# Layer 1 of a four-layer graph network: gate operations that read their scores in PSUM, and one-hots' buffers in another pool

## The chip, the cores and the metric

The kernel runs on one core of a Trainium2 chip. The core has a matrix engine (TensorE, PE in the profile; its weight loads are the rows PEld), a vector engine (VectorE, DVE), a scalar engine (ScalarE, ACT), a general engine (GpSimd, POOL) and a queue engine that starts DMA transfers (SyncE, SP). Each engine works through its own instructions in order, and engines wait for each other by semaphores. SBUF is the on-chip memory that all engines and the DMA read and write; PSUM holds the matmuls' results and can be read and written by VectorE and ScalarE too. The metric is device time in microseconds (us), as a median over several executions. Times inside a profile come from one further execution with the profiler.

## The reference, cut to what matters

An array `x` of 8 batches, 2048 nodes and 64 features, in float32, goes through four layers, each `x = layernorm(x + GNN_k(x))`. Layers 0, 2 and 3 are graph products with the adjacency `adj` (2048 x 2048, rows normalised) and with weights; layer 1, which the change touches, is an attention over 64 hyperedges:

```
h    = x @ W
agg  = softmax over the hyperedge's nodes of leaky_relu(h @ a_node), applied to h   # [b, e, f]
beta = sigmoid((h @ a_gn)[node] + (agg @ a_ge)[hyperedge])
all_he = elu(beta * h + (1 - beta) * agg)                       # per node and hyperedge
coefs1 = softmax over a node's hyperedges of tanh(elu(agg) @ fcW + fcb) @ av
g        = sum over hyperedges of coefs1 * all_he
industry = (adj / deg) @ (x @ W_ind)
out = industry and g, mixed by a softmax over tanh(. @ fcW + fcb) @ av
x   = layernorm(x + out)
```

A node belongs to few hyperedges, three on average: one drawn, and each of the others with a probability of 3%.

## The kernel before

**Data.** Rows are cut into 16 tiles of 128 nodes (`NT` = 16, `P` = 128); a tile holds all batches and features side by side, 8 x 64 = 512 columns (`BC`). The adjacency lies as 0/1 masks in DRAM scratch, 1 MB for a tile, and comes back through SP as `mj_l1_<tile>`. A product with it is 16 x 2 matmuls of 128 x 512 for a tile (line L1399 in layer 1), since the operand is split into a high and a low part.

**Stages.** The first product of layer 0 also prepares, beside its matmuls, what layer 1 needs of the hyperedges: for each tile four one-hot matrices `oh` (slots 0 to 3 of a node: which hyperedge it holds), a matrix `S` for what does not fit in slots, and `pT`, all stored to DRAM. Layer 0 follows, with weights that differ by node; then layer 1; then layers 2 and 3.

**Layer 1's beginning.** One pool, `l1`, lives through the whole layer (`S`, `agg1`, `nagg`, `ext` and small constants). A second pool, `fa`, holds what the beginning alone needs (`pT`, `agg`, `he`, `rec` and others); it is closed, and the memory after it goes to the pools `fw` (small tiles of the units, allocated by `small`) and `mjp` (two masks). A tile of `fw` or `mjp` can therefore be loaded only after the last reader of what lay at its address. The beginning loads `pT` and `S` in four parts each (`S` through SP behind a flag that VectorE computes at L1451, which decides between this program and a general one), forms `agg` (L537) and a copy of it in two parts (L545 is one of these copies), the scores of hyperedges with matmuls and exponentials (L575, L578 and L579 are small VectorE operations on [128 x 8] of them), sums into `ext`, a product `dnp` with `pT`, and last `hgr`, two numbers per node and batch: the node's part of the gate, and the reciprocal of the softmax's sum (L599). The part of tile 0's `industry` that can be done early runs on TensorE between these steps.

**Units.** `units(j)` computes `g` of tile j. It loads `oh` (L632, buffers for 4 tiles), and forms scores in one PSUM bank, `sm`: four matmuls one-hot x `ext` (L636), one of `S` x `hgr` (L640) and a transpose of `S` (L154). So each of the 80 score columns is a sum or a product partner for a slot u, a kind k (0: gate, 1: coefficient) and a batch. ScalarE copies the transpose to `ST` (L647) and the 80 columns to `ex` in SBUF (L649). VectorE makes `gate` (kind 0, add) and `coef` (kind 1, multiply), two operations each: slots 0 to 2 with `hgr` (24 columns, L654) and the last slot from two columns of `ex` (8 columns, L658). ScalarE turns `gate` into `sig` and `rest` (step `tau`, L661 to L665). POOL multiplies `h` by `sig` (L680, `ch0`, `ch1`), TensorE looks up `agg` with the one-hots (`gp0`, `gp1`, L693), VectorE multiplies that by `rest` and adds (`z`: L700, L703), ScalarE takes exp (L705) and a product for the last slot (`t3`, L718, eight small ones), VectorE forms the elu `ez` (`e`, L723), POOL multiplies by `coef` and sums (`w` and `ga`: L725, L729, L731), and a matmul with `ST` adds the last slot (`red`, L734; L736).

**Industry and mixer.** `industry(j)` is the 32 matmuls with the mask, steps `i`, and then `ind` (L754) and `dlt` (L758). `mix_and_norm(j)` transposes `g` and `ind`, multiplies by `fcW` (`fc0`, `fc1`, L793), takes tanh (`th0` L788, `th1` L796), subtracts (`sub`, L798), multiplies by `av` (`df`, L802, 16 matmul instructions of one column), and from there weights, residual and layernorm follow (`sw` L808, `mult` L810, `r` L814, `s` L817, `centre` L819, `sq` L824, `var` L827, `rstd`, `x2` L835). `df` and the scores of a unit take turns in the same PSUM bank.

**Order.** Everything on PE, VectorE, ScalarE and POOL in layer 1 runs in the order in which it is written (`program_order()`). The turns interleave tiles by a list written by hand. In turn t, `p` is the industry of tile t, `q` its end for tile t-1, `u` the unit of tile t+1, `v` the first steps of unit t+2, `s` the end of unit t, and `m`, `o`, `f` the mixers of tiles t-1, t-2, t-3:

```
"q.ind u.gp0 u.z0 q.dlt m.xg m.tr0 v.sx m.sT0 v.ST u.exp0 u.ch1 m.fc0 m.tr1 u.dp "
"o.mult m.sT1 p.i m.th0 f.rstd u.t3 u.e0 p.i o.r m.fc1 v.gates u.w0 o.s u.gp1 p.i "
"v.tau p.i m.th1 u.z1 s.ga p.i v.ch0 u.exp1 m.sub u.e1 o.centre s.red u.w1 f.x2 p.i "
"m.df s.g o.sq m.sw o.var p.i p.i"
```

So on VectorE the order around the gates is: `r` of tile t-2, the gates of unit t+2, `s`, z1 of unit t+1, `sub` of tile t-1. On TensorE, `df` stands behind six of the eight pairs of `industry`. Before turn 0 the units 0 and 1 are filled in ("the fill"). DMAs are not in this order: SP's instructions are placed by the framework's scheduler.

Of the kernel before, what the change touches and what calls it, by code (L numbers as in the profile page):

```python
# [8 lines left out]
F32 = mybir.dt.float32  # L9
# [8 lines left out]
B, N, C, E, D, K, J = 8, 2048, 64, 64, 16, 3, 128  # L18
P = 128
# [32 lines left out]
def kernel(  # L52
# [28 lines left out]
    nc = tc.nc  # L81
# [420 lines left out]
    def layer1(  # L502
# [7 lines left out]
        l1 = stack.enter_context(tc.tile_pool(name="fl1", bufs=1))  # L510
# [104 lines left out]
        def small(tag, name, shape=(P, B), bufs=2):  # L615
            return fw.tile(list(shape), F32, tag=tag, name=name, bufs=bufs)
# [10 lines left out]
        def units(j, dst):  # L627

            oh = small("oh", f"oh_{j}", (P, 4, P), 4)
            nc.sync.dma_start(oh, lists["oh"][j // 4][:, j % 4])  # L632
            sm = ps_s.tile([P, QW], F32, tag="sm", name=f"sx_{j}")

# [10 lines left out]
            yield "sx"  # L645
            ST = small("ST", f"ST_{j}", (P, P), 3)
            nc.scalar.copy(ST, sm[:, 0:P])  # L647
            ex = small("ex", f"ex_{j}", (P, 5, 2, B))
            nc.scalar.copy(ex.rearrange("p u k b -> p (u k b)"), sm[:, P:P + 80])  # L649
            yield "ST"  # L650
            gate = small("gate", f"gate_{j}", (P, 4, B))
            coef = small("coef", f"coef_{j}", (P, 4, B), 3)
            for t, k, op in ((gate, 0, ALU.add), (coef, 1, ALU.mult)):
                nc.vector.tensor_tensor(  # L654
                    t[:, 0:3, :], ex[:, 0:3, k, :],
                    hgr[:, j, k, :].unsqueeze(1).to_broadcast([P, 3, B]), op,
                )
                nc.vector.tensor_tensor(t[:, 3, :], ex[:, 3, k, :], ex[:, 4, k, :], op)  # L658
            yield "gates"

            nc.scalar.activation(gate, gate, AF.Tanh, scale=0.5)  # L661
# [217 lines left out]

        g_of, ind_of, dlt_of = {}, {}, {}  # L880
        unit = {j: units(j, g_of) for j in range(NT)}
        mixer = {j: mix_and_norm(j) for j in range(NT)}
        product = {j: industry(j) for j in range(NT)}
# [1247 lines left out]
```

## Time and profile before

| what | value |
|---|---|
| median of 3 runs | 1344.24 us (1344.21, 1344.24, 1349.38) |
| profiled execution | 1349.78 us, its span 1347.8 us |
| TensorE clock granted, mean | 0.96 |
| busy, share of the span | PE 95%, PEld 75%, VectorE 68%, ScalarE 28%, POOL 36% |
| layer 1, in the profiled execution | from about 734 to 1072 us, turns of 16.9 us each in the middle |
| one turn in there, busy | VectorE 15.3 us, POOL 13.0 us, ScalarE 11.3 us |

The profiled execution is one execution; its span begins with the first instruction, and about 2 us of its time lie around the span. In a row of a profile's timeline stand the start and the length in us, the engine, the line, the operation with what it writes and reads, its size, and in brackets the idle time of the engine ahead of it with the operation that ended it. "SPq" rows are SP's waits ahead of a DMA. The chain of waits goes back from the last instruction, each step to what released it. "x8" after a row means eight instructions of the kind, taken together.

### The profile page before, as it was taken

To read this page: it belongs to the slowest core of one execution; us is meant where nothing else is said; L and a number is where in the kernel's file an instruction comes from. 1 tells how busy PE (TensorE), PEld (TensorE's weight loads), DVE (VectorE), ACT (ScalarE), POOL (GpSimd) and SP (SyncE) were. 2 spreads that over 40 slices of the span, in tenths; PEclk is the share of its full clock that TensorE was granted. 3 is DMA by queue.
4 is the path that set the end of the run, shared out by engine and by line. 5 is a ranking of instruction groups with operands and counts; after the bars stand their busy time and mean duration, and the time that the engine had idled before them with its cause. 6 is when DMAs were issued, how large, how long until landed. Compare 5 with 4: busy or idle time off the path is not lost.

```text
span 1347.8 us, 19945 instructions
## 1 busy us (share of the span) xinstructions
PE 1275.1 (95%) x7708; PEld 1010.0 (75%) x7708; DVE 915.7 (68%) x1559; ACT 370.7 (28%) x853; POOL 483.8 (36%) x403
## 2 busy tenths in 40 slices
PE   6999899999999999999997599999998799999997
PEld 5777688888888888888885376666666588888885
DVE  3556378787877777777663669899984646655454
ACT  2100101111222222222212446666664511111111
POOL 2000354444444444444210667777772600000000
PEclk9999899999999999999997599999998999999999
DMA  8976632333333333331604022222220133333451
GB/s 219 269 215 182 197 112 89 104 105 104 105 104 105 105 105 105 105 105 55 256 23 152 24 75 77 91 95 94 79 78 1 49 140 125 125 120 139 171 188 72
DMA packets 100358, 157.21 MB, mean 117 GB/s; under 512 B 12832, under 2 KB 64416, under 8 KB 94112
## 3 DMA queue, kind: packets, MB, share of 16 engines
q1 hardware_dynamic: 97776, 151.65, 34.7%
q10 hardware_dynamic: 2304, 4.20, 0.8%
q8 instruction: 63, 1.03, 0.3%
q14 instruction: 39, 0.32, 0.1%
q0 software_dynamic: 176, 0.02, 0.1%
HBM read 118.08 MB, written 37.76 MB: 116 GB/s over the span
## 4 chain that ended last, share of the span: by engine, by line
PE 77%; DVE 14%; DMA 3%; ACT 2%; issue 1%; POOL 1%; SPq 0%; DVEq 0%; ACTq 0%; POOLq 0%
PE pp L1081 25%; PE a L1399 18%; PE y2p L1044 9%; PE y1p L478 7%; PE ind L1399 4%; DVE d L703 3%; PE df L802 2%; DMA xraw<-in_xn 2%; DVE gp L700 2%; DVE gate L654 2%; DVE ez L723 1%; PE try L154 1%; PE yp L1489 1%; DVE coef L658 1%; DVE th L798 1%
## 5 line engine op out<-in xcount | busy, mean ns | idle before, releaser
L1092 DVE SCALAR_TENSOR_TENSOR r<-pp,emb_sb,r 128x256 f32<-128x256 f32 x512 | 247.2, 483 | 114.9 <-PE pp L1081 101.1
L1081 PE MATMUL pp<-w_sb,xT 64*128 64x256 f32 x1024 | 160.4, 390 | 1.7 <-DVE r L1092 1.7
L1030 POOL TENSOR_TENSOR r<-xs,bn 128x256 f32<-128x256 f32 x32 | 22.7, 731 | 384.8 <-issue 245.3
L1081 PE MATMUL pp<-w_sb,y1T 64*128 64x256 f32 x1024 | 153.5, 376 | 0.0
L1081 PE MATMUL pp<-w_sb,y2T 64*128 64x256 f32 x1024 | 153.5, 376 | 0.0
L478 PE MATMUL y1p<-x_hi,m 128*128 128x512 f32 x256 | 105.9, 414 | 12.0 <-ACT x_hi L425 11.6
L1081 PEld LDWEIGHTS pp<-w_sb,xT 64*128 64x128 f32 x1024 | 94.4, 186 | 25.1 <-issue 14.9
L1081 PEld LDWEIGHTS pp<-w_sb,y1T 64*128 64x128 f32 x1024 | 99.7, 187 | 10.9
L1081 PEld LDWEIGHTS pp<-w_sb,y2T 64*128 64x128 f32 x1024 | 99.6, 187 | 11.0
L1399 PE MATMUL a<-y_hi,mj_l 128*128 128x512 f32 x256 | 102.9, 402 | 5.0 <-DMA mj_l<-mask 5.0
L1399 PE MATMUL ind<-y_hi,mj_l 128*128 128x512 f32 x240 | 104.8, 437 | 0.0
L1044 PE MATMUL y2p<-y_hi,msk 128*128 128x512 f32 x256 | 103.4, 404 | 0.0
L1399 PE MATMUL a<-y_lo,mj_l 128*128 128x512 f32 x256 | 102.7, 401 | 0.0
L478 PE MATMUL y1p<-x_lo,m 128*128 128x512 f32 x256 | 102.6, 401 | 0.0
L1044 PE MATMUL y2p<-y_lo,msk 128*128 128x512 f32 x256 | 101.5, 396 | 0.0
L1399 PE MATMUL a<-v_hi,mj_l 128*128 128x512 f32 x256 | 100.1, 392 | 0.0
L1399 PE MATMUL a<-v_lo,mj_l 128*128 128x512 f32 x256 | 100.0, 391 | 0.0
L1399 PE MATMUL ind<-y_lo,mj_l 128*128 128x512 f32 x240 | 96.7, 403 | 0.0
L725 POOL TENSOR_TENSOR ez<-ez,coef 128x1024 f32<-128x1024 f32 x32 | 69.9, 2184 | 71.3 <-DVE ez L723 69.0
L986 POOL TENSOR_TENSOR ms<-msk,srow 128x1024 f32<-128x1024 f32 x32 | 89.9, 2810 | 5.2 <-DVE ms L999 5.2
L478 PEld LDWEIGHTS y1p<-x_hi,m 128*128 128x128 f32 x256 | 49.3, 192 | 24.8 <-ACT x_hi L425 12.0
L978 DVE TENSOR_SCALAR msk<-adj 128x1024 fp32r<-128x1024 f32 x32 | 63.7, 2024 | 3.9 <-DMA adj<-in_at 3.8
(273 smaller groups left out, 2430.5 us busy)
## 6 DMA issues: line engine op xcount, KB each, us to landing
mj_l<-mask SPq DMA_DIRECT2D x47, 1024.0 KB, 4.9
raw<-in_at SPq DMA_DIRECT2D x32, 512.0 KB, 5.5
adj<-in_at SPq DMA_DIRECT2D x64, 256.0 KB, 3.6
mask<-msk SPq DMA_DIRECT2D x32, 512.0 KB, 4.4
xraw<-in_xn SPq DMA_DIRECT2D x8, 512.0 KB, 5.5
oh<-oh SPq DMA_DIRECT2D x32, 128.0 KB, 2.6
xT<-in_xt SPq DMA_DIRECT2D x16, 256.0 KB, 3.1
xs<-in_xn SPq DMA_DIRECT2D x16, 256.0 KB, 2.9
```

The lines of the kernel that those rows point to most:

```text
L478: nc.tensor.matmul(accs[q][jj], r_(m[:, t, jj * P:(jj + 1) * P]), r_(part[:, mt, :]), start=i + h + t == 0 and part is x_hi, stop=i == 3 a ...
L654: nc.vector.tensor_tensor(t[:, 0:3, :], ex[:, 0:3, k, :], hgr[:, j, k, :].unsqueeze(1).to_broadcast([P, 3, B]), op,)
L700: nc.vector.tensor_tensor(by_b(gp[:, 0:n]), by_b(gp[:, 0:n]), per_b(rest, 2 * i, n), ALU.mult)
L703: nc.vector.tensor_tensor(d, d, gp, ALU.add)
L725: nc.gpsimd.tensor_tensor(by_b(ez), by_b(ez), per_b(coef, 2 * i, 2), ALU.mult)
L802: nc.tensor.matmul(df[:, b:b + 1], th[:, b % 2, (b // 2) * P:(b // 2 + 1) * P], av_sb, start=True, stop=True,)
L978: nc.vector.tensor_scalar(r_(m), raws[j][h], 0.0, None, op0=ALU.is_gt)
L986: nc.gpsimd.tensor_tensor(ms, m, srow[j].unsqueeze(1).to_broadcast([P, 8, P]), ALU.mult)
L1044: nc.tensor.matmul(acc, r_(msk[j, mt // 8][:, mt % 8, :]), r_(part[:, mt, :]), start=mt == 0 and part is y_hi, stop=mt == NT - 1 and part ...
L1081: nc.tensor.matmul(pp[:, h, pl, :], terms[j][name][rs, 2 * bq + pl], w_sb[rs, k, dq * 4 * C:(dq + 1) * 4 * C], start=k == 0, stop=k == K - 1,)
L1092: nc.vector.scalar_tensor_tensor(rb, ppv[:, :, dd, :], emb_sb[:, j, d:d + 1], rb, op0=ALU.mult, op1=ALU.add)
L1399: nc.tensor.matmul(acc, r_(a[:, mt, :]), r_(part[:, mt, :]), start=mt == 0 and part is hi, stop=mt == NT - 1 and part is lo,)
```

## The change

Two edits, both in `units`. The 80 scores are no longer copied to SBUF by ScalarE; `ex` is now a view of the PSUM bank, and the gate operations read it there. Since the last slot's operation had two operands from `ex`, one of them is now copied to SBUF first, by VectorE, into the place of the result: there are six VectorE operations for four (line numbers of the new kernel: L653, L657, L658). And `oh` is allocated in the pool `l1`, with its four buffers, in place of `fw`; its memory is thus not shared with `fa`, and that of the later tiles moves.

```
-            oh = small("oh", f"oh_{j}", (P, 4, P), 4)
+            oh = l1.tile([P, 4, P], F32, tag="oh", name=f"oh_{j}", bufs=4)
             nc.sync.dma_start(oh, lists["oh"][j // 4][:, j % 4])
...
             ST = small("ST", f"ST_{j}", (P, P), 3)
             nc.scalar.copy(ST, sm[:, 0:P])
-            ex = small("ex", f"ex_{j}", (P, 5, 2, B))
-            nc.scalar.copy(ex.rearrange("p u k b -> p (u k b)"), sm[:, P:P + 80])
             yield "ST"
             gate = small("gate", f"gate_{j}", (P, 4, B))
             coef = small("coef", f"coef_{j}", (P, 4, B), 3)
+            ex = sm[:, P:P + 80].rearrange("p (u k b) -> p u k b", u=5, k=2)
             for t, k, op in ((gate, 0, ALU.add), (coef, 1, ALU.mult)):
                 nc.vector.tensor_tensor(
                     t[:, 0:3, :], ex[:, 0:3, k, :],
                     hgr[:, j, k, :].unsqueeze(1).to_broadcast([P, 3, B]), op,
                 )
-                nc.vector.tensor_tensor(t[:, 3, :], ex[:, 3, k, :], ex[:, 4, k, :], op)
+                nc.vector.tensor_copy(t[:, 3, :], ex[:, 4, k, :])
+                nc.vector.tensor_tensor(t[:, 3, :], ex[:, 3, k, :], t[:, 3, :], op)
             yield "gates"
```

The framework's scheduler, which places the DMAs, moves some of SP's instructions as well: `pT`'s four loads ahead of two pieces of tile 0's mask, the first four `oh` directly behind `S`, and the mask of tile 1 (`mj_l1_1`) behind the reciprocal L599, since its memory now overlaps that of `rec`. On VectorE `agg` (L537) comes ahead of the flag's operations (L1449 to L1451).

More of the change, by code (lines that the diff above doesn't have):

```diff
@@ L627, in units @@
         def units(j, dst):
-            oh = small("oh", f"oh_{j}", (P, 4, P), 4)
+            oh = l1.tile([P, 4, P], F32, tag="oh", name=f"oh_{j}", bufs=4)
             nc.sync.dma_start(oh, lists["oh"][j // 4][:, j % 4])
@@ L647, in units @@
             nc.scalar.copy(ST, sm[:, 0:P])
-            ex = small("ex", f"ex_{j}", (P, 5, 2, B))
-            nc.scalar.copy(ex.rearrange("p u k b -> p (u k b)"), sm[:, P:P + 80])
             yield "ST"
@@ L652, in units @@
             coef = small("coef", f"coef_{j}", (P, 4, B), 3)
+            ex = sm[:, P:P + 80].rearrange("p (u k b) -> p u k b", u=5, k=2)
             for t, k, op in ((gate, 0, ALU.add), (coef, 1, ALU.mult)):
@@ L657, in units @@
                 )
-                nc.vector.tensor_tensor(t[:, 3, :], ex[:, 3, k, :], ex[:, 4, k, :], op)
+                nc.vector.tensor_copy(t[:, 3, :], ex[:, 4, k, :])
+                nc.vector.tensor_tensor(t[:, 3, :], ex[:, 3, k, :], t[:, 3, :], op)
             yield "gates"
```

## The prediction

> **What bounds the kernel now.** I read the page's first part, then the chain of work that ended last in order of time (start, length, work), then the timeline of one turn of layer 1.
>
> ```profile
> PE 1275.1 (95%) x7708; PEld 1010.0 (75%) x7708; DVE 915.7 (68%) x1559; ACT 370.7 (28%) x853; POOL 483.8 (36%) x403
> 735.89 4.21 DMA oh<-oh
> 760.74 1.81 DVE coef L658
> 783.95 1.84 PE L802 MATMUL df<-av_sb,th 128*128 128x1 f32 x16
> 854.93 3.38 PE ind L1399 x8
> 915.04 1.80 DVE gate L654
> 921.94 1.95 PE df L802 x16
> 923.89 1.96 PE ind L1399 x8
> ```
>
> TensorE bounds the span, but in layer 1 (734 to 1072 us) the chain leaves it: a load of one-hots at the beginning, a gate operation of VectorE later. The fourth line is from the timeline, for use below. Now one turn in steady state:
>
> ```profile
> 914.59 2.21 POOL L725 TENSOR_TENSOR ez<-ez,coef 128x1024 f32<-128x1024 f32 x1 [1.62 <-DVE ez L723]
> 914.96 1.88 DVE L654 TENSOR_TENSOR gate<-ex,hgr 128x24 f32<-128x24 f32 x1
> 916.77 0.15 DVE L658 TENSOR_TENSOR gate<-ex 128x8 f32<-128x8 f32 x1
> 916.84 0.17 DVE L654 TENSOR_TENSOR coef<-ex,hgr 128x24 f32<-128x24 f32 x1
> 916.88 1.30 POOL L729 TENSOR_TENSOR g<-ez 128x512 f32<-128x512 f32 x1
> 916.94 1.26 DVE L658 TENSOR_TENSOR coef<-ex 128x8 f32<-128x8 f32 x1
> 919.38 1.91 POOL L680 TENSOR_TENSOR d<-h,sig 128x1024 f32<-128x1024 f32 x1
> 919.53 1.22 DVE L703 TENSOR_TENSOR d<-d,gp 128x1024 f32<-128x1024 f32 x1
> 921.11 0.40 PE L1399 MATMUL ind<-y_lo,mj_l 128*128 128x512 f32 x1
> 921.94 1.95 PE L802 MATMUL df<-av_sb,th 128*128 128x1 f32 x16 [0.44 <-DVE th L798]
> ```
>
> Two gate operations of 24 and 8 columns take 1.88 and 1.26 us where their like take 0.17, and each ends with a POOL operation (914.59 + 2.21 = 916.80, 916.88 + 1.30 = 918.18): VectorE with two operands in SBUF waits while POOL reads SBUF. L703, with one operand in PSUM (gp), runs beside POOL in its usual 1.22. So the gates' 0.43 us (L654 begins 773.30, the last L658 ends 773.73, when POOL is away) become 3.24. The `sub` operation (L798) then ends late, and df waits for it: the matmuls before it start 0.233 apart, so df could start at 921.34 and starts at 921.94.
>
> **The change, part by part.**
> 1. *Gates read PSUM.* Out go 16 copies by ScalarE (0.23 us each). They hide: in a turn ScalarE is busy 11.28 of 16.9 us, and after the copy at 927.68 it waits 1.03 us for VectorE. Worth nothing. VectorE gets six operations for four, two of which wait for the copy ahead of them. Start to start is 0.09 us without a wait and 0.21 with one (the pair L578, L579 at 728.62 and 728.83): 0, 0.09, 0.30, 0.39, 0.48, 0.69, end 0.86 us, so 0.43 more than four operations unblocked, but 2.38 less than now. Does reading PSUM cost more? The small row L575 (from PSUM) takes 0.17 us, L578 (from SBUF) 0.17: no. [...]
>    No row shows a copy from PSUM beside POOL. Bounds: 0.16 us, or up to the end of POOL's operation (as 1.88 now). A copy SBUF to SBUF here takes 0.42 us for 512 columns (L545)[...] I take 0.16, the row of L575.
> 2. *Does the turn become shorter?* With times of the turn above: gates 914.96 to 915.82; `s` (0.68) to 916.4; L700 (0.68) must wait for the gp1 matmuls (916.19 + 0.72), so 916.95 instead of 918.72; L703 (1.22) to 918.97; its th1 from ScalarE is done by 917.95 (fc1 ends 916.26, tau after t3 to 916.9, then 1.07); sub (1.22) from 918.9 to 920.1. df can take it at 921.34: 1.2 us of slack, so the wait is gone whole. What is late next? Nothing on TensorE: gp0, at 925.1 then, needs ez done by 921.5; POOL's work (13.0 us a turn) also moves up 1.8 us. The turn becomes TensorE's own: 16.88 - 0.60 = 16.28. The waits of df behind its preceding matmul, less 0.233, in turns 2 to 13: ten of 0.58 to 0.61, one of 0.47, one of 0.58, sum 7.0 us. Turn 1 has none (783.95), its gates being unblocked. **7.0 us.**
>    In the fill, coef (760.66, 1.89 us) holds L700 from 761.9, when its matmuls are done, to 762.47: **0.6 us**. At 753.11 the same block hides behind POOL's L680, which ends 756.8. Gate tanh starts with the third operation, 0.1 to 0.2 us later for units 0 and 1: unit 0's is on the path, **-0.1**.
> 3. *One-hots in layer 1's own pool.* Now their four first loads wait on SP until VectorE's last operation in the shared memory:
>
> ```profile
> 733.57 0.95 DVE L599 RECIPROCAL hgr<-rec 128x128 f32<-128x128 f32 x1
> 734.58 27.58 SPq L632 DMA_DIRECT2D oh<-oh  x6
> 738.31 1.00 PE L636 MATMUL sx<-ext,oh 128*128 128x16 f32 x4 [5.66 <-DMA oh<-oh]
> 739.16 0.59 PE L640 MATMUL sx<-hgr,S 128*128 128x16 f32 x2
> ```
>
>    In the program after, the loads come after S's four on SP with no wait on VectorE of their own. S waits for the flag (VectorE, about 720.5, with `agg` now ahead of the flag); four S (0.58 each) and four one-hots then go out to about 725.5 and land in 2.6 us, 728. The L636 matmuls need them at 732.7, after dnp, so those four go beside the ScalarE and VectorE steps to hgr, and L640 starts at 734.6 (hgr at 734.52) instead of 739.16. **4.5 us**, all of it on the chain, since up to 775 each step waits for the one ahead.
>    What else moves on SP: pT's four loads go out near 670, ahead of two pieces of the early mask, which are needed from 702; their memory's last reader is VectorE's compare at 665.5. The mask load for turn 1 (1 MB, 4.9 us) moves from 713.61 to behind hgr, 734.6, since its memory now overlaps `rec`; with the second it is there by 745, and its matmuls come at 771. Behind it on SP waits the fifth one-hot, which waits for gp1 of unit 0 anyway. Both free.
> 4. *Clock.* Three times TensorE ran at half clock for some us after df (the 854.93 row: 3.38 us for 8 matmuls, 1.96 usually), about 1.5 us each, all in turns where df waited. With the waits gone they may go (4.5) or stay (0; turns change length, so stretches without a wait could dip too, even +1.5). The nearest rows, nine turns with a wait and no dip, say that a wait alone isn't the cause: I take one dip, **1.5 us**. TensorE's return to full clock in the fill (776.0) comes in steps of 3.4 us (the clock record), at half speed worth up to 0.9 either way: 0.
>
> Sum: 7.0 + 0.6 - 0.1 + 4.5 + 1.5 = 13.5 us. The profiled execution took 1349.78 (span 1347.8 and 2.0 around it); it becomes 1336.3. It lies 5.5 above the median of 1344.24, near the third run (1349.38); carried over, the forecast is 1331 (1330.7).
>
> **Rivals.**
> - *Only the beginning pays.* Something lies just behind sub: fc1 already waits on ScalarE's th0 (it ends at 914.72, fc1 starts at 915.13). For it: TensorE's chain gp0 to fc1 is as long as the ScalarE/VectorE chain beside it. Against: that chain starts from gp0 and moves with TensorE. 1344.2 - 5.0 = 1339, no change by measurement.
> - *Only the turns pay.* S or one-hots land late, after 734.5, because the SP queue is held by the early waits. Against: seven us of margin. 1344.2 - 7.6 = 1336.6.
> - *Slower.* The copies from PSUM do wait for POOL, and lose each time to the next operation in POOL's queue (L725, L729, L731). Gates then last over 4.2 us: sub is 0.93 later than now, which over 12 turns (11.2) outweighs the 4.5 won plus 6.7. With three POOL operations waited out (1.26 more, and 0.43 for the extra operations) it's 12 x 1.69 - 4.5 = +16: 1360. Against: L575's row[...]. A wait on just two, as now, gives 12 x 0.43 - 4.5 = +0.7, no change.
> - *All dips go too:* 3 us more, 1328.
>
> **How the numbers follow.** 0.5% is 6.7 us, about what a measurement of this kernel can tell from no change; faster means under 1337.5. Both parts pay (1327.5 to 1335): 0.62. All dips go: 0.08. Only turns: 0.09. Those three are faster: 0.79. Only the beginning, or copies that wait twice: 0.16, same. Slower: 0.05. Range 1326.5 to 1339.5: the cases from all dips gone to only the beginning; outside lie the slower case and the edges.
>
> **What would show it.** Right: L653, L657 and L658 at 0.15 to 0.18 us each beside POOL; no DVE entry for gate in the chain; df 0.23 us after the matmul ahead of it; df to df 16.3 us; the first L640 straight behind the reciprocal L599; S and one-hot loads before 726. Wrong: L657 at over 1 us; df still waiting on L798 or on something new; the first sx still waiting on a DMA; a mask load late for turn 1.

## The result, and the profile after

The changed kernel takes 1329.47 us (median of 4 runs, 1328.12 to 1332.58) against 1344.43 before (4 runs): a ratio of 0.9884, 95% interval 0.9857 to 0.9910. A second set, with 20 runs of the kernel before (1345.72, 1340.37 to 1351.03) and 5 of the changed one, gives 1326.50 and 0.9860 (0.9836 to 0.9885). So 15 to 19 us are gone; the traces below show 19.8 for layer 1. The profiled execution of the changed kernel took 1332.58 us, its span is 1330.5.

From the page of the changed kernel, the busy shares and the shares of the chain that ended last; the last line has the chain's shares before:

```profile
PE 1265.6 (95%) x7708; PEld 1006.4 (76%) x7708; DVE 885.8 (67%) x1591; ACT 368.9 (28%) x837; POOL 484.3 (36%) x403
PE 88%; DMA 3%; DVE 3%; ACT 2%; issue 1%; POOL 1%; SPq 0%; DVEq 0%; ACTq 0%; POOLq 0%
PE 77%; DVE 14%; DMA 3%; ACT 2%; issue 1%; POOL 1%; SPq 0%; DVEq 0%; ACTq 0%; POOLq 0%
```

VectorE has 32 instructions more (1591 for 1559) and is busy 29.9 us less, since the gate operations no longer stand in waits that count as busy time. In the chain VectorE falls from 14% to 3%, and TensorE rises from 77% to 88%.

The turn whose rows of before the prediction showed, now in the timeline of the changed kernel (start, length, engine, line, operation; in brackets the engine's idle time ahead of it):

```profile
918.89 2.21 POOL L725 TENSOR_TENSOR ez<-ez,coef 128x1024 f32<-128x1024 f32 x1 [2.61 <-DVE ez L723]
919.26 0.18 DVE L653 TENSOR_TENSOR gate<-sx,hgr 128x24 f32<-128x24 f32 x1
919.36 0.16 DVE L657 COPY gate<-sx 128x8 f32<-128x8 f32 x1
919.55 0.17 DVE L658 TENSOR_TENSOR gate<-sx,gate 128x8 f32<-128x8 f32 x1
919.63 0.17 DVE L653 TENSOR_TENSOR coef<-sx,hgr 128x24 f32<-128x24 f32 x1
919.72 0.16 DVE L657 COPY coef<-sx 128x8 f32<-128x8 f32 x1
919.91 0.17 DVE L658 TENSOR_TENSOR coef<-sx,coef 128x8 f32<-128x8 f32 x1
921.26 0.70 DVE L700 TENSOR_TENSOR gp<-gp,rest 128x512 f32<-128x512 f32 x1 [0.59 <-PE gp L693]
923.23 1.22 DVE L798 TENSOR_TENSOR th<-fc,th 128x1024 f32<-128x1024 f32 x1
925.38 0.40 PE L1399 MATMUL ind<-y_lo,mj_l 128*128 128x512 f32 x1
925.38 1.99 PEld L802 LDWEIGHTS df<-av_sb,th 128*128 128x128 f32 x16
925.61 1.84 PE L802 MATMUL df<-av_sb,th 128*128 128x1 f32 x16
```

All six gate operations lie inside one POOL operation (918.89 to 921.10) and take 0.16 to 0.18 us each. They end 0.82 us after they began, 3.24 before. `sub` (L798) ends at 924.45; `df` begins 0.23 us after the matmul ahead of it began, with nothing in brackets. So `sub` is 1.16 us early where it was late, and `df`'s first weights are loaded ahead of it (PEld, 925.38).

The beginning, in the same trace:

```profile
724.85 1.85 SPq L632 DMA_DIRECT2D oh<-oh  x4
734.92 1.02 PE L636 MATMUL sx<-ext,oh 128*128 128x16 f32 x4
735.91 0.95 DVE L599 RECIPROCAL hgr<-rec 128x128 f32<-128x128 f32 x1
736.92 0.61 PE L640 MATMUL sx<-hgr,S 128*128 128x16 f32 x2 [0.98 <-DVE hgr L599]
737.01 0.80 SPq L1394 DMA_DIRECT2D mj_l<-mask  x2
```

The one-hots' loads go out at 724.85, the matmuls with them (L636) run beside the steps to `hgr`, and L640 follows the reciprocal by 0.06 us. The two masks start behind it, as foreseen, and nothing waits for them.

The stretches of layer 1 in the traces, each measured between two starts:

| stretch | before | changed | difference |
|---|---|---|---|
| `dnp` (L588) to first L640 | 10.06 | 5.47 | -4.59 |
| L640 to `df` of turn 1 | 44.79 | 43.36 | -1.43 |
| `df` of turn 1 to `df` of turn 14 | 223.39 | 209.92 | -13.47 |
| `df` of turn 14 to the next adjacency product's first matmul | 70.35 | 70.08 | -0.27 |
| sum | 348.59 | 328.83 | -19.8 |

The spans differ by less (17.3 us), because `dnp` itself began 2.35 us later in the changed kernel's profile. That is no effect of the change: over the profiles of all kernels here `dnp` begins between 723.6 and 731.7 us, the latest two being of the changed kernel, the earliest of `pad_2` below, whose edit lies behind that point.

### The profile page after: what moved, and what is told of

The parts are those of the page before. It is cut to its first block, busy times and chain, and to the rows that moved or that the text cites. A ratio compares the mean times of both kernels' runs of the same rounds, so it can differ in the third digit from the quotient of the medians.

```text
span 1330.5 us, 19952 instructions
## 1 busy us (share of the span) xinstructions
PE 1265.6 (95%) x7708; PEld 1006.4 (76%) x7708; DVE 885.8 (67%) x1591; ACT 368.9 (28%) x837; POOL 484.3 (36%) x403
## 4 chain that ended last, share of the span: by engine, by line
PE 88%; DMA 3%; DVE 3%; ACT 2%; issue 1%; POOL 1%; SPq 0%; DVEq 0%; ACTq 0%; POOLq 0%
PE pp L1081 25%; PE a L1399 18%; PE y2p L1044 9%; PE ind L1399 8%; PE y1p L478 7%; PE fc L793 3%; PE df L802 2%; DMA xraw<-in_xn 2%; PE gp L693 1%; PE try L154 1%; PE yp L1489 1%; PE trm L154 1%; PE hp L1169 1%; PE aggp L1201 1%; PE sgp L1148 1%
## 5 line engine op out<-in xcount | busy, mean ns | idle before, releaser
L1399 PE MATMUL ind<-y_hi,mj_l 128*128 128x512 f32 x240 | 101.7, 424 | 0.0
L725 POOL TENSOR_TENSOR ez<-ez,coef 128x1024 f32<-128x1024 f32 x32 | 69.9, 2184 | 56.2 <-DVE ez L723 54.8
```

Source lines behind the costliest of these rows:

```text
L725: nc.gpsimd.tensor_tensor(by_b(ez), by_b(ez), per_b(coef, 2 * i, 2), ALU.mult)
L1399: nc.tensor.matmul(acc, r_(a[:, mt, :]), r_(part[:, mt, :]), start=mt == 0 and part is hi, stop=mt == NT - 1 and part is lo,)
```

## The experiments

Theory: an operation of VectorE with two operands in SBUF waits while POOL works on SBUF (1.88 and 1.26 us for the gates beside L725 and L729, 0.16 and 0.17 with POOL away at 773.30), and so does a copy from SBUF to SBUF, which no row of before shows; with an operand in PSUM it doesn't (L703, 1.22 beside L680); through `sub` these waits held `df`; and the late one-hots held the first unit. Rivals: the gates were held by ScalarE's copy; only one of the two parts pays; the turns were bound by VectorE's amount of work.

**The halves, and both kernels once more.**

```
start_only: only   oh = l1.tile([P, 4, P], F32, tag="oh", ..., bufs=4)
gates_only: the change, with   oh = small("oh", f"oh_{j}", (P, 4, P), 4)   put back
after_again, before_again: no edit
```

> Gates from PSUM as in the change; one-hots stay in the pool fw. If the two parts are independent and the gates pay by themselves (VectorE no longer waits for POOL): turns of 16.15 us from df to df, no wait of df on sub, gate operations of 0.16 to 0.18 us each, and the first L640 late again, behind its one-hots' load; the time is that of the change plus the beginning's 4.6 us, about 1334 (ratio 0.992). If only the beginning pays and the shorter turns come from elsewhere: about 1344 (ratio 1.00). If the gates need the beginning (a mask or one-hot later on): turns between 16.15 and 16.88.

> One-hots in the pool l1; scores still copied by ScalarE and gates in SBUF as before. If the parts are independent: L640 straight behind the reciprocal L599, 4.6 us earlier against dnp than before; turns stay 16.88 us, gate operations of 1.8 and 1.3 us beside POOL; time about 1344.4 - 4.6 = 1339.8 (ratio 0.9966). If the earlier start is lost again in the fill: 1344 (1.00). If the one-hots' place has to do with the turns too: under 1336.

> The changed kernel once more, beside the two halves: 1329 (ratio 0.989), the sum of the two halves' gains within 2 us if they are independent. Its trace shows whether dips of the clock inside the turns come back in another execution: none if they hang on df's wait, some if they come by chance.

> The kernel before once more, one look. The first profile had three turns of about 18.3 us in place of 16.88, at half clock behind df, 4.7 us in all, and lay 5.5 us above the median. If those dips are chance of that execution, this one near the median has none or one and takes about 1344; if they belong to the kernel, three again and about 1349.

| kernel | median us (runs) | ratio (95%) | `df` to `df` | `dnp` to L640 |
|---|---|---|---|---|
| start_only | 1339.57 (15) | 0.9957 (0.9940 to 0.9975) | 16.88, two of 18.47 | 4.31 |
| gates_only | 1332.58 (6) | 0.9906 (0.9883 to 0.9928) | 16.10 to 16.16 | 10.19 |
| after_again | 1326.50 (5) | 0.9860 (0.9836 to 0.9885) | 16.11 to 16.16 | 5.47 |
| before_again | 1343.22 (1) | | 16.88, two of 18.4 | 10.15 |

The halves gain 6.1 and 13.1 us, the whole 19.2: they add up, each known to some 3 us. In the timeline of gates_only the first unit still waits for its load, which still stands behind L599:

```profile
728.72 0.95 DVE L599 RECIPROCAL hgr<-rec 128x128 f32<-128x128 f32 x1
729.74 1.74 SPq L632 DMA_DIRECT2D oh<-oh  x4
733.60 0.99 PE L636 MATMUL sx<-ext,oh 128*128 128x16 f32 x4 [5.79 <-DMA oh<-oh]
```

and in the chain of start_only the gates still stand in every turn at the lengths of before:

```profile
835.99 1.80 DVE gate L654
837.96 1.18 DVE coef L658
842.89 1.95 PE df L802 x16
```

start_only's 4.31 us hold 1.16 of gain that come from TensorE's clock: from `dnp` to L636 it took 2.31 us, the changed kernel 3.47 (731.45 to 734.92), with the same matmuls. The granted clock was still 1.00 when start_only's `dnp` began (725.87, until 727.15) and 0.50 during that of the changed kernel (from 730.92). Without that the part is worth 4.6 to 4.7 us in start_only too, against 10.06 and 10.15 before.

**Where the operands lie.**

```
six_in_sbuf: the change, with ScalarE's copy of the 80 columns put back:
+            ex = small("ex", f"ex_{j}", (P, 5, 2, B))
+            nc.scalar.copy(ex.rearrange("p u k b -> p (u k b)"), sm[:, P:P + 80])
...
-            ex = sm[:, P:P + 80].rearrange("p (u k b) -> p u k b", u=5, k=2)
four_one_psum: the change, with
+            ex4 = small("ex4", f"ex4_{j}", (P, 2, B))
+            nc.scalar.copy(ex4.rearrange("p k b -> p (k b)"), sm[:, P + 64:P + 80])
...
-                nc.vector.tensor_copy(t[:, 3, :], ex[:, 4, k, :])
-                nc.vector.tensor_tensor(t[:, 3, :], ex[:, 3, k, :], t[:, 3, :], op)
+                nc.vector.tensor_tensor(t[:, 3, :], ex[:, 3, k, :], ex4[:, k, :], op)
```

> The changed kernel with ScalarE's copy of the 80 scores back, so that the six gate operations have all their operands in SBUF; one-hots stay in l1. If an operation with two operands in SBUF waits for POOL and that is the whole matter: the first operation ends with L725 (about 1.9 us), a later one with L729 (1.3 us), a third wait for the copy is possible; sub is 0.4 us or more later than before the change, turns of 17.3 us or longer, dips of the clock come back (2 or 3 of 1.5 us), about 1326.5 + 13 x 1.15 + 3 = 1344 or more. If the place of the operands doesn't matter and the change only spared something else (six for four, or another order): turns of 16.15 us, 1327.

> The changed kernel with four gate operations: ScalarE copies only the 16 columns of the last matmul to SBUF, each gate operation has one operand in PSUM and one in SBUF, no copy by VectorE. If two SBUF operands are what waits: all four at 0.17 us beside POOL, turns of 16.15 us, time as after, 1326.5 to 1329.5. If the wait on ScalarE's copy was what cost: turns near 16.88, about 1339. If one SBUF operand is enough to wait: the same.

six_in_sbuf takes 1418.45 us (4 runs), a ratio of 1.0541 (1.0511 to 1.0571): the same six operations with the same counts, 92 us slower than the changed kernel. Where they read is what differs; ScalarE's copy ahead of them is in start_only too, at 1339.57. Its timeline, one turn (its lines stand one or more later: L654, L658, L659 are the changed kernel's L653, L657, L658; L726, L730, L732, L681 are L725, L729, L731, L680):

```profile
925.35 2.21 POOL L726 TENSOR_TENSOR ez<-ez,coef 128x1024 f32<-128x1024 f32 x1 [4.27 <-DVE ez L724]
925.72 1.88 DVE L654 TENSOR_TENSOR gate<-ex,hgr 128x24 f32<-128x24 f32 x1
927.52 0.16 DVE L658 COPY gate<-ex 128x8 f32<-128x8 f32 x1
927.64 1.30 POOL L730 TENSOR_TENSOR g<-ez 128x512 f32<-128x512 f32 x1
927.72 1.24 DVE L659 TENSOR_TENSOR gate<-ex,gate 128x8 f32<-128x8 f32 x1
928.88 0.17 DVE L654 TENSOR_TENSOR coef<-ex,hgr 128x24 f32<-128x24 f32 x1
928.89 1.32 POOL L732 TENSOR_TENSOR g<-g,ez 128x512 f32<-128x512 f32 x1
928.97 1.27 DVE L658 COPY coef<-ex 128x8 f32<-128x8 f32 x1
930.18 1.89 POOL L681 TENSOR_TENSOR d<-h,sig 128x1024 f32<-128x1024 f32 x1
930.28 1.82 DVE L659 TENSOR_TENSOR coef<-ex,coef 128x8 f32<-128x8 f32 x1
```

The gates lose to four POOL operations in a row: each operation that begins 0.08 to 0.37 us after POOL's ends with it (927.60, 928.96, 930.24 and 932.10, POOL's 927.56, 928.94, 930.21 and 932.07). Even a copy of 8 columns takes 1.27 us. The gates last 6.4 us, turns in the middle 22.7 to 23.7, `df` waits 2.9 to 3.7 us, and nine of the twelve `df` behind these waits take 3.17 to 3.58 us in place of 1.95 (granted clock 0.82 from 780 to 1000 us, 0.98 in before; mean of the run 0.938, 0.968 in that of the change). It expected 1344 "or more"; the number of lost races was underestimated, not their kind.

four_one_psum takes 1327.00 us (0.9860, 0.9830 to 0.9890). Its four gate operations take 0.15 to 0.17 us beside POOL, turns are 16.18. One operand in SBUF beside one in PSUM does not wait for POOL, and ScalarE's copy was not what cost: it is back, in part, at no price. This also does without the two copies that the changed kernel gives to VectorE. The four operations of POOL that held VectorE both read and write SBUF; which of the two it is, no run separates. Not every operation of POOL did: beside L831 (8 columns, 911.30 to 912.97 in before) L810, with both tensors in SBUF, took its usual 0.68 us (912.61).

**How late `sub` may be.**

```
             nc.vector.tensor_reduce(s, b_view(r), AX.X, ALU.add)
+            for i in range(2):                         # pad_4: range(4)
+                pad = small("pad", f"pad_{j}_{i}")
+                nc.vector.tensor_reduce(pad, b_view(r), AX.X, ALU.add)
             yield "s"
```

> The changed kernel with two repeats of the reduction s (L817) behind s in each turn, 0.60 us each from start to start, one operand in SBUF, result unused. In the trace of after L700 waits 0.59 us for gp1's matmuls and sub ends 1.16 us before df can start: 1.75 us of slack against 1.2 added. If TensorE alone bounds the turn: 16.15 us, time as after. If VectorE's order is already at its limit: 16.7 to 17.3 us, 1334 to 1341.

> The same with four repeats, 2.4 us, as long as the gate operations' waits for POOL were before the change (3.24 - 0.80). With 1.75 us of slack sub comes 0.65 us late, df waits for it, and loses the 0.11 us that a weight load ahead of time saved: turns of 16.9 us, as before the change, 13 x 0.76 = 10 us, without any wait for POOL. If dips of the clock hang on df's wait, 2 or 3 turns of 18.4 us come back, about 1326.5 + 10 + 3 = 1339 to 1341; if they hang on VectorE waiting for POOL, none, about 1337.

pad_2, with 1.2 us more of VectorE in each turn, has turns of 16.20 us and no wait at `df`; 1330.93 us (0.9893, 0.9862 to 0.9923). pad_4 has turns of 16.82 and takes 1340.05 (18 runs; 0.9959, 0.9941 to 0.9977). Its timeline:

```profile
920.80 2.46 DVE L820 TENSOR_REDUCE pad<-r 128x8 f32<-128x512 f32 x4
925.13 1.22 DVE L798 TENSOR_TENSOR th<-fc,th 128x1024 f32<-128x1024 f32 x1
926.40 1.86 PEld L802 LDWEIGHTS df<-av_sb,th 128*128 128x128 f32 x16 [0.80 <-DVE th L798]
926.40 1.95 PE L802 MATMUL df<-av_sb,th 128*128 128x1 f32 x16 [0.37 <-DVE th L798]
```

The gates are those of the change, 0.15 to 0.18 us each, without a wait for POOL; only `sub` is late. From the first `df` to the fourteenth 11.3 us are lost again, of 12.0 (against before_again) to 13.5 (against before) that the change had won there. So the gates mattered through `sub` and `df`, as the prediction had it. VectorE's amount of work alone bounds nothing with 1.2 us more, and by the rows of the changed kernel up to about 1.75 (1.16 ahead of `df` and L700's idle 0.59).

pad_4 also brought the clock's dips back, two of them. From its chain, a turn with one and a turn without:

```profile
908.02 2.04 PE df L802 x16
910.06 3.44 PE ind L1402 x8
926.40 1.95 PE df L802 x16
928.35 1.97 PE ind L1402 x8
```

Eight matmuls take 3.44 us in place of 1.97 behind a `df` that had waited, and the turn takes 18.38. Over the profiles of before, before_again, start_only and pad_4, 48 turns had a wait of `df`, and 9 of them a dip (3, 2, 2, 2). Over the seven profiles without such waits (the changed kernel twice, gates_only, four_one_psum, pad_2 and the two below) 91 turns had none.

Which of the 48 dip goes by a grid in the traces' clock records: there the granted clock changes only at points 3.413 us apart, and each dip is one step of this grid at a granted clock of 0.50. Before's `df` at 852.83, which had waited 0.59 us, began in the step from 851.06 to 854.48; 2.23 us of that step were wait or `df`, and the next step ran at half clock. Its `df` at 835.95 had waited 0.60 us, but only 2.06 us of wait and `df` fell into one step (834.00 to 837.41), and no dip followed. The same sum for every turn, with 1.81 us for a `df` that waited and 1.70 for one that didn't:

| most of wait and `df` within one step, us | turns | dips |
|---|---|---|
| 2.13 to 2.42 | 9 | 9 |
| 1.17 to 2.08, `df` had waited | 39 | 0 |
| up to 1.71, `df` had not waited | 91 | 0 |

So the border lies between 2.08 and 2.13 us of a step, an estimate for this sequence of matmuls from these 48 turns. That the wait and `df`'s one-column matmuls count alike is an assumption that fits all 48. `df` without a wait, at 1.70 us, stays below the border wherever it falls, and with these waits the change took away all dips, not some. Where the grid lies differs from execution to execution (a point at 851.06 us in before's profile, at 850.39 in that of the change), and with it which turns dip.

**A faster fill.** Up to the first `df` each step waits for the one ahead, so two more edits were tried there:

```
fill_both:
-                nc.scalar.copy(rec, dn[:, :, 0, :])
...
-                nc.vector.reciprocal(hgr[:, :, 1, :], rec)
+                for ts in (slice(0, 1), slice(1, NT)):
+                    nc.scalar.copy(rec[:, ts], dn[:, ts, 0, :])
...
+                    nc.vector.reciprocal(hgr[:, ts, 1, :], rec[:, ts])
...
-            run(unit, 0, second)
-            run(unit, 1, first)
+            run(unit, 0, "gp0 z0 exp0 ch1 dp t3 e0 w0 gp1")
+            run(unit, 1, "sx ST")
+            run(unit, 0, "z1")                         # fill_exp: "z1 exp1"
+            run(unit, 1, "gates tau ch0")
+            run(unit, 0, "exp1 e1 w1")                 # fill_exp: "e1 w1"
```

> The changed kernel with two more edits ahead of turn 0: the reciprocal and the three small steps before it are done for tile 0's column first and for the other 15 tiles after, and unit 1's scores, gates and first POOL product are issued between the steps of unit 0 instead of behind them. If each step up to turn 0 waits for the one ahead (as the 4.6 us of the one-hots' loads suggest): the first L640 comes 0.9 us earlier behind dnp than the 5.47 us of after, unit 1's L703 no longer waits for POOL (about 1.4 us), 2.3 us together up to the first df, 1324 to 1327. If another chain lies close behind (POOL's products, or the mask of tile 1): 0 to 1 us up to the first df, 1326 to 1329. Slower if unit 1's operations stand in front of unit 0's: the first df later than 48.8 us behind dnp.

> The kernel fill_both with one step moved: exp1 of unit 0 (ScalarE) is issued ahead of unit 1's gates and tau. In fill_both that exponential stood ready at 743.25 us and began at 744.15, behind tau, so 0.85 us of what the new order won was lost. If that is all: 0.85 us earlier from unit 0's gp1 to unit 1's gp0 (5.9 in place of 6.7), about 46.4 us from dnp to the first df at the clock of fill_both; time 1323.5, which can't be told from 1324.3. If POOL's product of unit 1, now later, comes to stand in front of unit 0's last one: nothing won, 47.2 us.

fill_both takes 1324.28 us (0.9852, 0.9824 to 0.9879), fill_exp 1327.32 (0.9874, 0.9852 to 0.9896): neither can be told from the changed kernel's 0.9860. The traces show what moved. L636 to L640 fell from 2.00 to 1.07 us, as expected. From L640 to unit 1's second `gp` (L693) the changed kernel needs 21.52 us, fill_both 21.63, fill_exp 20.81: in fill_both ScalarE's exponential stood behind unit 1's `tau`, as fill_exp then showed (unit 0's `gp1` to unit 1's `gp0` 5.84 us for 6.70). From there to the first `df` both lost (0.4 and 0.75 us): the next pair of `gp` matmuls took 1.19 us, what such a pair takes at a granted clock of 0.50 (758.44 in the changed kernel's profile), where it took 0.71 at 1.00 there (764.41). So fill_exp won 1.6 us up to there (0.9 ahead of L640, 0.7 behind it) and gave nearly half of it back; neither order of the fill yielded more.

## Why the prediction was right, point by point

Forecast were 1331.0 us and a gain of 13.3 on the median; measured were 1329.47 and 15.0, in the larger set 1326.50 and 19.2, at the range's lower end. The sum was 13.5 us where layer 1's traces show 19.8 (beginning 4.6, fill 1.4, turns 8.8, dips 4.6, end 0.3). Its terms in turn:

- *Gates.* Right: six operations in 0.82 us (0.86 forecast), each at the row of L575 (0.15 to 0.18 us); start to start 0.08 to 0.10 without and 0.19 with a wait (0.09 and 0.21). The direct comparison is in six_in_sbuf, whose first unit has POOL idle: the same six operations from SBUF last 0.84 us there (730.84 to 731.68), in the changed kernel's first unit from PSUM 0.82 (738.21 to 739.03). An extra cost of PSUM does not show for these shapes. The open bound, a copy from PSUM beside POOL, was taken at its lower end: the author's estimate, from L575's row alone, which has no POOL beside it. L657's 0.16 us beside POOL is that end. six_in_sbuf shows how far away the upper end was: had operands in PSUM waited like those in SBUF, the "slower" rival's price of 16 us above the kernel before would have been 72 (1418.45 against 1346.47).
- *Slack.* Right: 1.2 us forecast, 1.16 measured, and the pads found its end between 1.2 and 2.4 us of added work (1.75 with L700's idle time).
- *The turn's length.* Forecast 16.28 us, measured 16.15: 0.73 off each turn, not 0.60. The term that was left out is `df` itself. When `th` came late, `df`'s first weight load started together with its first matmul (pad_4 shows it at 926.40); now the weights are loaded ahead (925.38 for 925.61), and from the start of `df` to the next matmul pass 1.70 us for 1.81. That leaves 0.02 open. Over 12 turns 8.8 us, not 7.0.
- *Dips.* This step failed in size: one dip, 1.5 us, was taken to go; all three of the profile went, 4.6 us with the third behind turn 13 (the other profile of the kernel before has two). The argument was that nine waits without a dip show a wait not to be the cause. They show only that a wait is not sufficient: the nine dips had 2.13 us or more of wait and `df` in one step of the clock's grid, the 39 waits without a dip 2.08 or less. A wait is necessary, as far as the runs go (9 dips in 48 turns with a wait, none in 91 without), and taking away a necessary condition takes away all. The rival "all dips go" (1328) describes the traces.
- *Fill.* Right: `gp` to `gp` in unit 1's end 6.57 to 5.97 us, the 0.6 forecast; the later tanh costs 0.09 (0.1 forecast).
- *Beginning.* Right: 4.59 us (4.5 forecast), and start_only has it alone.
- *The clock's return in the fill*, set at 0 with 0.9 either way, came out at 0.9 of gain in this execution: from unit 2's first `gp` to the first `df` 15.87 us (764.41 to 780.28), before 16.76. It goes both ways: start_only, with the gates of before, is 1.1 faster than before from L640 to `df`, and the fill kernels lost 0.4 and 0.75 there to the changed kernel.
- *The offset of the profiled execution.* 5.5 us above the median were carried over whole. The 20 runs spread over 1340 to 1351, so one execution's place says little about the next kernel's; that the changed kernel's profiled execution also lay 3.1 above its median was luck. So was how near the number came: the terms were 6.3 us short in the traces, the gain 5.9 short in the larger set, and only 1.7 in the first set with its four runs.

Of the rivals, "only the beginning" is refuted by gates_only, "only the turns" by start_only, "slower" by the 0.16 us of L657.

## What to carry to other kernels

When a VectorE operation takes many times as long as its like and ends with an operation of POOL, look at where its operands lie before changing the order: one operand in PSUM freed it here (0.15 to 0.17 us for up to 1.88), and a small copy by another engine "to have it in SBUF" cost 0.7 us per turn without being waited for in a turn. A wait's price isn't only its length: count also what the stalled engine could have prepared (a weight load, 0.11 us here) and what its clock does behind the stall (3.44 us for 1.97 in a dip). And a condition that isn't sufficient can still be necessary: cases where it stood without the effect don't say that the effect stays when the condition goes.

## What was not expected of the hardware

A copy of 8 columns from SBUF to SBUF on VectorE took 1.27 us beside POOL, 0.16 from PSUM. In a row of small operations each can lose to the next POOL operation: four in a row in six_in_sbuf, 6.4 us for 0.8 us of work.

A wait of 0.5 to 0.6 us ahead of matmuls of one column came with TensorE's granted clock at 0.50 for one step of 3.4 us in 9 of 48 cases, and the place of the grid decided which (2.13 us or more of wait and `df` in one step; none at 2.08 or less). TensorE was idle for at most 0.44 us ahead of these dips: a step that was only partly idle was enough here, when at least 1.5 us of the rest went to `df`.
